# Values of all batches projected as their distinct context rows: three row sets in place of four batches, a layout by transfers, and a new order of the beginning

## The chip, the core and the metric

The kernel is one program on one core of a Trainium2 chip. A core has a matrix engine (PE, with its weight loads PEld shown apart), a vector engine (DVE), a scalar engine (ACT), a general engine (POOL) and a queue engine (SP), which here only starts transfers. Each of them works through its own list of instructions in order and meets the others at semaphores. The metric is the device time of one launch in microseconds (us), the median of several runs.

## The reference

Cross attention with a residual and a layer normalisation: 4 batches of 2048 query rows, 77 context rows per batch, width 512, 16 heads of 32.

```python
qs  = (q @ wq).reshape(Bq, Lq, H, HD).transpose(0, 2, 1, 3)      # q: (4, 2048, 512)
ks_ = (k @ wk).reshape(Bq, Lk, H, HD).transpose(0, 2, 1, 3)      # k = v = context: (4, 77, 512)
vs  = (v @ wv).reshape(Bq, Lk, H, HD).transpose(0, 2, 1, 3)
scores = jnp.einsum('bhqd,bhkd->bhqk', qs, ks_) / jnp.sqrt(jnp.float32(HD))
scores = jnp.where(mask[:, None, :, :], -jnp.inf, scores)
attn_w = jax.nn.softmax(scores, axis=-1)
attn = jnp.einsum('bhqk,bhkd->bhqd', attn_w, vs).transpose(0, 2, 1, 3).reshape(Bq, Lq, H * HD)
out = attn @ wo + q
mu = jnp.mean(out, axis=-1, keepdims=True)
var = jnp.mean((out - mu) ** 2, axis=-1, keepdims=True)
return (out - mu) / jnp.sqrt(var + EPS) * gamma + beta
```

## The kernel before

The 8192 query rows are 64 tiles of 128 rows. Two tiles make a block (256 rows, 32 of them), four make a group (512 rows, 16 of them). All large products are made in three passes of a format with fewer bits: each operand is cast (the high part, on ACT) and the rest is taken off it (the low part, on DVE or POOL), and high·high, low·high and high·low are added up in one PSUM bank. One product of 128 x 128 by 128 x 512 over a contraction of 512 is therefore 12 matmuls.

Nothing is scheduled by a compiler. The text `ORDER` is a list of some 2090 words, and the program emits the work in the order of these words, so that each engine gets its own words in their order. A word is a letter and a number. The letters that matter here:

- `A`, `C`, `F`: load the value weights wv in four slabs (SP), cast them while they are transferred (a transfer that POOL starts), take the low part (DVE). `R`, `p`, `G`: the same for the output weights wo, which take over the buffers `woh` and `wol` once the keys are projected with wk from them. `g`, `l`, `i`, `j`: load half a group of transposed x (`xT`), cast it on ACT (`xth`, L259), take its low part on POOL (`xtl`, L263).
- `H`, `Q`: projections of queries (L269); a `Q` is 12 matmuls of 512 columns, `I` and `q` copy the result out on DVE (L283, L285). `K`, `J`: copies of projected keys out of PSUM to `kct`, on ACT (L305) and on DVE (L307).
- `B`: values of one batch, 12 matmuls (L325). `D`: their copy out of PSUM (L332).
- `S`: scores of a tile, 64 small matmuls (L388). `T`: maxima of four heads with the mask's bias (DVE, L405). `e`: four exponentials and their sums (ACT, L420). `r`, `n`, `t`: reciprocals (DVE), scaling (POOL, L435), transposition in blocks of 32 (DVE, L456, into `B`).
- `P`: one of 12 transfers that regroup a block's transposed probabilities from `B` to `PT` (SP, L467). `V`: their product with the values of the block (L481). `a`, `b`: high and low part of it (ACT L510, DVE L514). `x`: load of the rows of x for the residual, `O`: the output projection (L534), `+`, `s`, `v`, `k`, `f`, `w`: residual, moments, the root (POOL), scale (ACT), the affine part (POOL), the store.

The second text, `SLOTS`, names the buffer that each tile takes, tag by tag: "mm" are the 8 PSUM banks, "o" the 8 row buffers, "xth" and "xtl" the two buffers of cast x.

A block's probabilities stand on 96 partitions: 77 keys for the even head of a pair and 77 for the odd one, the odd one's last 19 shifted in front or behind, so that a block of 32 is shared. The context is therefore loaded with its last 19 rows a second time (96 columns for each batch). The values are projected from these 96 columns, one batch at a time, and each copy out of PSUM multiplies the rows by a column of zeros and ones (`vm`, made at the start by `value_rows`): in the even heads the rows from 77 on are zero, in the odd ones the rows 58 to 76.

```python
def values_evac(b, a):
    pv = vd[b][:NK2].rearrange("p (q a d) -> p q a d", a=2, d=HD)
    vv = vsb[:, b].rearrange("p (q a d) -> p q a d", a=2, d=HD)
    nc.vector.tensor_scalar(vv[:, :, a], pv[:, :, a], vm[:, a, 0:1], None, ALU.mult)
```

The kernel ahead of the words (all of it in the listing below) loads the first rows of x, wq, the context and wk, projects the first 256 query rows and the keys; the words begin when the keys are projected. From tile 18 on the words repeat in a pattern of one block: two scores, one product with values, two projections of queries and two output projections.

Of the kernel before, what the change touches and what calls it, by code (L numbers as in the profile page):

```python
# [17 lines left out]
P = 128  # L18
# [13 lines left out]
GRP = 2 * BLK  # L32
MASKED = -3.38e38
# [5 lines left out]
LATE = 48  # L39

# [3 lines left out]
A0 A1 A2 A3 E l0 l2 C0 C1 C2 C3 g4 R2 g5 x1 J1 R1 M1.3 H2 K0 R3 p J3 K2 Y1 M0.1 R0 i2 i3 j2 S1 I2 S0 T1.1 e1.1 T1.3  # L44
j3 H0 T0.2 e0.2 T0.0 T0.1 e0.1 M8.4 F2 Q6 T0.3 e0.3 T1.2 I0 e0.0 T1.0 Q5 q6 i4 F0 r0 F3 e1.0 n0 S2 q5 e1.3 S3 T2.1
T2.3 j4 e1.2 Q4 t0 i5 F1 g6 Q7 r1 M4.4 T2.0 n1 T3.1 T3.3 e3.3 B2 j5 t1 e2.0 T3.0 P0.7s e3.1 P0.4s B1 D2.1 g7 G0
e3.0 x3 G1 x5 q4 P0.3s e2.3 T2.2 x4 B0 D1.0 P0.5s q7 i6 P0.6s M12.4 G2 e2.1 P0.9s D1.1 j6 P0.1s T3.2 S4 e2.2 D0.0
P0.2s T4.2 B3 P0.0s i7 r2 T4.1 P0.8s n2 e3.2 T4.0 P0.10s T4.3 P0.11s S5 e4.3 D3.0 g8 t2 Q11 x7 e4.0 L1 D2.0 T5.0
e4.2 r3 D0.1 n3 Q8 q11 e4.1 T5.1 D3.1 T5.2 e5.0 Q9 q8 T5.3 e5.3 r4 G3 t3 n4 e5.1 S6 P1.10s T6.3 V0 e6.3 P1.0s j7 q9
P1.8s T6.0 e5.2 P1.5s T6.1 S7 P1.6s T6.2 Q10 a0.0 t4 P1.2s e6.0 P1.9s P1.7s T7.3 a0.1 P1.3s e6.2 r5 T7.1 n5 Q13 x0  # L50
b0.1 P1.4s T7.2 e7.2 b0.0 t5 e6.1 O1 T7.0 P2.5s i8 q10 P1.1s q13 e7.0 P1.11s S8 P2.9s +1 r6 e7.1 P2.4s S9 T8.0 n6
P2.6s T8.2 O0 P2.8s e7.3 T8.3 P2.10s T8.1 g9 e8.1 t6 Y0 P2.11s Q15 P2.7s T9.2 e9.2 P2.0s T9.0 P2.1s r7 T9.1 n7 e8.3
P2.2s +0 V1 P2.3s s1 e8.2 T9.3 j8 t7 S10 a1.0 e8.0 Q12 b1.0 P3.2s T10.0 e9.3 x2 q15 P3.7s s0 P3.10s a1.1 Q14 e9.1
P3.8s r8 T10.3 v0 P3.3s T10.1 g11 e9.0 n8 T10.2 x6 b1.1 P3.11s O3 q12 e10.0 P3.4s r9 n9 t8 k0 e10.3 q14 V2 +3 f0 t9
a2.0 S11 a2.1 b2.0 k1 P4.5s O2 T11.1 P3.9s i9 T11.3 P4.11s e10.1 T11.2 j9 P3.5s b2.1 P4.9s e11.3 O5 P3.6s +2 P3.0s
s3 f1 e11.1 s2 M16.4 e10.2 S12 +5 T12.0 Q16 e11.2 v1 w1 r10 T12.1 P3.1s T12.3 n10 g10 k2 s5 P4.0s k3 O4 P4.2s q16
e12.1 P4.10s T11.0 f3 P4.1s e11.0 P4.4s w0 V3 +4 P4.7s T12.2 e12.2 P4.3s r11 t10 n11 w3 S13 P4.6s a3.0 a3.1 Q17 s4
P4.8s e12.3 T13.2 f2 b3.1 e12.0 b3.0 t11 O6 i10 v2 T13.0 e13.2 P5.0s r12 P5.3s T13.1 n12 P5.1s k5 S14 P5.8s k4
T14.0 O7 x9 e13.0 T14.2 f5 P5.2s T13.3 P5.5s e14.0 q17 w2 +6 V4 +7 e13.3 j10 w5 s7 P5.4s T14.3 P5.10s S15 a4.1 t12
P5.7s e13.1 f4 Q19 P5.9s P5.6s a4.0 T15.2 e14.3 x8 s6 x11 b4.0 P5.11s v3 Q18 T15.3 x13 r13 T14.1 N x10 e14.1 n13  # L60
b4.1 q19 e14.2 O9 T15.0 T15.1 k7 t13 e15.3 f7 O8 q18 P6.7s r14 e15.0 w4 +9 P6.2s s9 P6.4s i11 n14 w7 S16 +8 k6
P6.10s e15.2 T16.1 V5 P6.6s j11 T16.0 P6.1s T16.2 e16.1 x12 s8 S17 P6.0s P6.3s a5.0 T16.3 v4 Q20 e15.1 P6.9s t14
P6.11s f6 k9 P6.8s T17.0 P6.5s a5.1 T17.2 Q21 e16.2 g12 r15 b5.1 x15 n15 b5.0 e16.3 T17.3 T17.1 O11 e16.0 M20.4 q21
f9 e17.0 t15 O10 e17.3 q20 P7.7s r16 w6 +11 n16 i12 P7.2s s11 P7.4s k8 S18 w9 +10 e17.2 j12 P7.10s T18.1 V6 P7.6s
# [80 lines left out]
        "03762310475304714356170247102743062152346501256043120647150"  # L145
    ),
    "q": "1010101010101010",
    "xth": "1010101010101010",
    "xtl": "1010101010101010",
    "xtf": "010101010110101010101010101010",  # L150
    "PT": "1010101010101010101010101010101010",
# [16 lines left out]
def xattn_layernorm(  # L168
# [373 lines left out]
    def residual(t):  # L542
        nc.vector.tensor_tensor(od[t], pos.pop(t), od[t], ALU.add)  # L543
# [186 lines left out]
```

## Time and profile before

| | |
|---|---|
| median of 3 runs | 521.2 us (521.06 to 522.1) |
| the profiled execution's own time | 521.43 us |
| its span | 519.4 us |
| granted clock of the matrix engine | 0.998 |
| busy: PE, DVE, ACT, POOL | 507.8, 480.3, 460.2, 406.0 us |
| matmuls of the values | 48, from 39.5 us to 51.8 us |
| first exponential | 23.02 us |
| scores of tile 18 begin | 148.33 us |

The profile's span runs from the first to the last instruction; 2.0 us of the execution's time lie outside it. Busy time of PE covers the pipelined duration of matmuls (about 0.39 us for 512 columns), not the distance at which they follow each other, so what a matmul costs is read from the chain of work, where 36 of them take 8.30 us.

### The profile page before, as it was taken

To read this page: it belongs to the slowest core of one execution; us is meant where nothing else is said; L and a number is where in the kernel's file an instruction comes from. 1 tells how busy PE (TensorE), PEld (TensorE's weight loads), DVE (VectorE), ACT (ScalarE), POOL (GpSimd) and SP (SyncE) were. 2 spreads that over 40 slices of the span, in tenths; PEclk is the share of its full clock that TensorE was granted. 3 is DMA by queue.
4 is the path that set the end of the run, shared out by engine and by line. 5 is a ranking of instruction groups with operands and counts; after the bars stand their busy time and mean duration, and the time that the engine had idled before them with its cause. 6 is when DMAs were issued, how large, how long until landed. Compare 5 with 4: busy or idle time off the path is not lost.

```text
span 519.4 us, 20351 instructions
## 1 busy us (share of the span) xinstructions
PE 507.8 (98%) x6857; PEld 389.0 (75%) x6857; DVE 480.3 (92%) x2587; ACT 460.2 (89%) x2215; POOL 406.0 (78%) x368
## 2 busy tenths in 40 slices
PE   8999999999999999999999999999999898999995
PEld 6986787777777777777777787777777676667673
DVE  5798999979999999999999999999999999999997
ACT  6689999998999999999999999999999899988410
POOL 0655536898988998988888998988889689787652
PEclk9999999999999999999999999999999999999999
DMA  8957479677687786877777787877878575876863
GB/s 303 398 186 184 131 176 224 173 203 229 182 226 210 220 231 196 212 236 207 224 223 211 214 228 200 235 210 223 233 196 238 146 204 146 245 204 191 245 210 148
DMA packets 58583, 110.38 MB, mean 213 GB/s; under 512 B 9392, under 2 KB 11056, under 8 KB 58480
## 3 DMA queue, kind: packets, MB, share of 16 engines
q1 hardware_dynamic: 55024, 102.27, 68.6%
q0 software_dynamic: 2496, 5.77, 4.0%
q8 instruction: 54, 0.88, 0.8%
q10 hardware_dynamic: 960, 1.05, 0.7%
q14 instruction: 49, 0.40, 0.3%
HBM read 41.94 MB, written 16.78 MB: 113 GB/s over the span
## 4 chain that ended last, share of the span: by engine, by line
PE 63%; DVE 22%; POOL 5%; DMA 4%; SPq 2%; issue 2%; ACT 1%; DVEq 0%; POOLq 0%
PE pq L269 26%; PE po L534 19%; PE sc L388 8%; PE pa L481 7%; DVE pbuf L405 5%; DVE B L456 5%; DVE AL L514 2%; PE pv L325 2%; DVE o L589 2%; DVE st L576 2%; DVE o L586 2%; PE pk L292 1%; POOL pbuf L435 1%; DVE o L543 1%; DMA stage_a<-wk 1%
## 5 line engine op out<-in xcount | busy, mean ns | idle before, releaser
L420 ACT ACTIVATE pbuf<-pbuf,nm 128x77 f32<-128x77 f32 x1024 | 352.6, 351 | 11.5 <-DVE nm L405 11.5
L420 ACT ACTIVATION_READ_ACCUMULATOR pbuf<-pbuf,nm 128x1 f32 x1024 | 196.0, 191 | 0.0
L405 DVE CUSTOM_DVE_ANT_0 pbuf<-sc,mb 128x77 f32<-128x77 f32 x1024 | 171.3, 232 | 9.2 <-PE sc L388 5.1
L435 POOL TENSOR_TENSOR pbuf<-pbuf,ri 128x1232 f32<-128x1232 f32 x63 | 143.1, 2272 | 37.8 <-DVE ri L430 37.2
L269 PE MATMUL pq<-xth,wqh 128*128 128x512 f32 (+1 forms) x256 | 101.7, 397 | 1.3 <-DVE nm L405 1.1
L534 PE MATMUL po<-woh,AH 128*128 128x512 f32 x256 | 102.5, 400 | 0.0
L534 PE MATMUL po<-woh,AL 128*128 128x512 f32 x256 | 100.0, 391 | 1.8 <-DVE AL L514 1.6
L534 PE MATMUL po<-wol,AH 128*128 128x512 f32 x256 | 99.7, 390 | 0.0
L269 PE MATMUL pq<-xtl,wqh 128*128 128x512 f32 (+1 forms) x256 | 98.3, 384 | 0.2 <-POOL rn L554 0.2
L269 PE MATMUL pq<-xth,wql 128*128 128x512 f32 (+1 forms) x256 | 98.1, 383 | 0.0
L456 DVE STREAM_TRANSPOSE B<-pbuf 128x1280 f32<-128x1280 f32 x64 | 96.1, 1502 | 1.5 <-DMA PT<-B 0.9
L405 DVE DVE_READ_ACCUMULATOR2_ANT nm<- 128x1 f32 x1024 | 84.4, 82 | 0.0
L263 POOL TENSOR_TENSOR xtl<-xtf,xth 128x1024 fp32r<-128x1024 f32 x28 | 67.4, 2406 | 6.0 <-ACT xth L259 6.0
L388 PEld LDWEIGHTS sc<-kct,q 32*64 32x64 f32 x4096 | 52.1, 130 | 24.6 <-issue 13.1
L568 POOL TENSOR_TENSOR o<-o,bet 128x512 f32<-128x512 f32 x48 | 62.6, 1305 | 3.8
L567 POOL TENSOR_TENSOR o<-o,gam 128x512 f32<-128x512 f32 x48 | 63.4, 1321 | 0.9 <-ACT o L563 0.8
L388 PE MATMUL sc<-kct,q 32*64 32x77 f32 x4096 | 62.1, 238 | 0.6 <-DVE nm L405 0.5
L481 PE MATMUL pa<-PT,vsb 96*32 96x256 f32 x992 | 60.0, 382 | 0.0
L269 PEld LDWEIGHTS pq<-xth,wqh 128*128 128x128 f32 x256 | 48.0, 188 | 13.4 <-DVE nm L405 1.5
L534 PEld LDWEIGHTS po<-woh,AL 128*128 128x128 f32 x256 | 48.0, 188 | 13.2 <-DVE AL L514 3.1
L534 PEld LDWEIGHTS po<-woh,AH 128*128 128x128 f32 x256 | 48.1, 188 | 12.0 <-issue 1.8
L534 PEld LDWEIGHTS po<-wol,AH 128*128 128x128 f32 x256 | 48.1, 188 | 10.5 <-issue 1.0
(96 smaller groups left out, 661.4 us busy)
## 6 DMA issues: line engine op xcount, KB each, us to landing
PT<-B SPq DMA_DIRECT2D x343, 128.0 KB, 2.9
o<-x SPq DMA_DIRECT2D x64, 256.0 KB, 4.0
out<-o SPq DMA_DIRECT2D x64, 256.0 KB, 3.0
xtf<-xT SPq DMA_DIRECT2D x28, 512.0 KB, 4.2
PT<-B POOLq DMA_DIRECT2D x25, 128.0 KB, 3.3
xtf<-xT SPq DMA_DIRECT2D x4, 256.0 KB, 5.8
stage_a<-wq SPq DMA_DIRECT2D x4, 256.0 KB, 4.7
stage_a<-wk SPq DMA_DIRECT2D x4, 256.0 KB
```

Of the source, the lines that this page charges most:

```text
L263: nc.gpsimd.tensor_tensor(l[:, c : c + 2], fx.pop((g, c)), xh[g][:, c : c + 2].bitcast(F32), ALU.subtract)
L269: nc.tensor.matmul(pq, w[:, c, m * P : (m + 1) * P], r[g][:, c, rs], start=(n == 0), stop=(n == 11))
L325: nc.tensor.matmul(pv[:NK2, :], ctx_s[c][i][:, b, :], v[c], start=(n == 0), stop=(n == 11))
L388: mm = nc.tensor.matmul(sc[j][r0 : r0 + SR, g * NK : (g + 1) * NK], qs[q, g, rs.start + r0 : rs.start + r0 + SR], kct[q, g, t // TPB, keys ...
L405: nc.vector.tensor_tensor_reduce(pb[:, h // 2, (h % 2) * NK : (h % 2 + 1) * NK], scs[t][j][:, g * NK : (g + 1) * NK], mb[:, t % TPB, keys_ ...
L420: nc.scalar.activation(pb[:, h // 2, (h % 2) * NK : (h % 2 + 1) * NK], pb[:, h // 2, (h % 2) * NK : (h % 2 + 1) * NK], AF.Exp, bias=nmax[t ...
L435: nc.gpsimd.tensor_tensor(pv, pv, rv.to_broadcast((P, NP, 2, NK)), ALU.mult)
L456: nc.vector.transpose(bt.rearrange("p c q r -> p q c r"), pbuf[t % NPB].rearrange("p q (c r) -> p q c r", c=5),)
L481: nc.tensor.matmul(pas[b, g // 2][HD * j : HD * (j + 1), (g % 2) * BLK : (g % 2 + 1) * BLK], vsb[:, 2 * b // TPB, HD * h : HD * (h + 1)], ...
L534: nc.tensor.matmul(pos[t], a[:, c, rs], w[:, c, :], start=(first and c == 0 and n == 0), stop=(c == NC_D - 1 and n == 2),)
L567: nc.gpsimd.tensor_tensor(o, o, gam, ALU.mult)
L568: nc.gpsimd.tensor_tensor(o, o, bet, ALU.add)
```

## The change

1. **Context.** It is loaded without the repeated rows: 308 columns (4 x 77) in place of 384. The keys are projected from these 308 columns in place of 312.
2. **Values.** The 308 rows are projected as three sets of 128, 128 and 52 rows: 36 matmuls in place of 48. The columns of wv are reordered on the host, so that the even heads stand first. A set is copied out of PSUM whole (`values_evac`, three copies of 512 columns in place of eight of 256), into a row buffer, and 14 transfers (`place`, word `Z`, on SP) bring the rows to the partitions and batches where they belong in `vsb`. Rows that must be zero are set by three memsets on POOL ahead of everything; the memsets and the transposition on DVE that made `vm` are gone.
3. **Order.** The words up to the scores of tile 18 are written anew. From there on each engine's words are the same, one for one, as before. The words ahead of that point are the same ones on each engine, except `D` and `Z`, but stand in another order: batch sets 0, 2, 1; tile 6 ahead of tile 5 and 9 ahead of 8; blocks 0 and 1 multiplied with their values one right behind the other, block 3 ahead of block 2.
4. **Row buffers at the end.** The last eight tiles' rows of x (`LAST = 56`) are loaded into the buffers of cast x in place of the row buffers "o".

Some new helpers in the file (`hold`, `residual_late`, `shift_one`, `scale_one`, and the letters `*`, `#`, `@`, `%`, `o`) are used by no word.

On SP, ahead of the first two products with values. `PT` is a block's regrouped probabilities, `o` a tile's rows of x, `vsb` the values, `v` a projected set. Before:

```order
L365 DMA m_1_947<-mask 128x1536
L467 DMA PT_1063<-B_926 32x2x512 x9
L519 DMA o_1206<-x 128x512
L467 DMA PT_1063<-B_926 32x2x512
L467 DMA PT_1243<-B_1166 32x2x512
```

and in the changed kernel, from the load of x ahead of block 1's transfers to the load of xT behind them:

```order
L533 DMA o_940<-x 128x512
L343 DMA vsb<-v_880 19x256
L343 DMA vsb<-v_776 58x512
L478 DMA PT_1010<-B_913 32x2x512 x7
L343 DMA vsb<-v_776 19x256
L478 DMA PT_1010<-B_913 32x2x512 x2
L343 DMA vsb<-v_776 19x256
L478 DMA PT_1010<-B_913 32x2x512 x3
L262 DMA xtf_2_1177<-xT 128x1024
```

Four placements, three of them of batch 0, now stand among the twelve transfers of block 1.

On ACT, at the first words. `kct` are the keys (from the banks `pk`, in which the four parts lie; the scores begin with the first part), `xth` the cast x, the last row the first exponentials. Before:

```order
L305 ACTIVATE kct<-pk_232 128x4x77
L305 ACTIVATE kct<-pk_232 128x4x19
L305 ACTIVATE kct<-pk_234 128x4x77
L305 ACTIVATE kct<-pk_234 128x4x19
L259 CAST xth_347<-stage_a 128x1024 x2
L420 ACTIVATE pbuf_81,sum_430<-pbuf_81,nm_425 128x77 x4
```

and in the changed kernel:

```order
L311 ACTIVATE kct<-pk_226 128x4x77
L311 ACTIVATE kct<-pk_226 128x4x19
L265 CAST xth_332<-stage_a 128x1024
L311 ACTIVATE kct<-pk_224 128x4x77
L311 ACTIVATE kct<-pk_224 128x4x19
L265 CAST xth_332<-stage_a 128x1024
L431 ACTIVATE pbuf_80,sum_421<-pbuf_80,nm_416 128x77 x16
```

The third part of the keys is now copied first, and the first part (224) behind a cast of x that waits for its load (the second half of group 1).

On POOL, ahead of the low part of group 5's second half (`xtl`, the last row of both), which the projections `Q20` and `Q21` read. Before:

```order
L435 TENSOR_TENSOR pbuf_81<-pbuf_81,ri_2260 128x8x154
L567 TENSOR_TENSOR o_941<-o_941,gam 128x512
L568 TENSOR_TENSOR o_941<-o_941,bet 128x512
L435 TENSOR_TENSOR pbuf_82<-pbuf_82,ri_2329 128x8x154
L263 TENSOR_TENSOR xtl_2141<-xtf_2_1574,xth_2008 128x1024
```

and in the changed kernel:

```order
L446 TENSOR_TENSOR pbuf_81<-pbuf_81,ri_2172 128x8x154
L587 TENSOR_TENSOR o_1989<-o_1989,gam 128x512
L588 TENSOR_TENSOR o_1989<-o_1989,bet 128x512
L587 TENSOR_TENSOR o_1877<-o_1877,gam 128x512
L588 TENSOR_TENSOR o_1877<-o_1877,bet 128x512
L587 TENSOR_TENSOR o_1947<-o_1947,gam 128x512
L588 TENSOR_TENSOR o_1947<-o_1947,bet 128x512
L446 TENSOR_TENSOR pbuf_82<-pbuf_82,ri_2334 128x8x154
L269 TENSOR_TENSOR xtl_1996<-xtf_2_2011,xth_1821 128x1024
```

Two more tiles' affine parts stand between the two scalings.

The diff, cut to its core:

```diff
+PLACES = []
+for b in range(4):
+    cuts = sorted({0, NK - TAIL_K, NK} | {k for k in range(NK) if (b * NK + k) % P == 0})
+    for k0, k1 in zip(cuts, cuts[1:]):
+        PLACES += [(b, k0, k1, a) for a in ((None,) if k0 < NK - TAIL_K else (0, 1))]
...
 ORDER = """
-A0 A1 A2 A3 E l0 l2 C0 C1 C2 C3 g4 R2 g5 x1 J1 R1 M1.3 H2 K0 R3 p J3 K2 Y1 M0.1 R0 i2 i3 j2 S1 I2 S0 T1.1 e1.1 T1.3
+R1 R0 R3 E l0 l2 C2 C0 C1 C3 g5 M4.4 A0 M0.1 M12.4 A1 M1.3 A3 M8.4 K2 A2 H2 J3 p i3 g4 J1 K0 i2 S0 I2 j2 S1 T0.1
...
     for c in range(NC_D):
             for w, i in ((woh, 0), (woh, 1), (wol, 0)):
                 nc.tensor.matmul(
-                    pks[m][:, : NB * (NK + 1)],
+                    pks[m][:, : NB * NK],
...
-    def values(b):
-        pv = bank(f"pv_{b}")
+    def value_zeros():
+        for a, z0 in ((0, 64), (1, 32), (1, 64)):
+            nc.gpsimd.memset(vsb[z0 : z0 + 32, :, a], 0.0)
+
+    def values(g):
+        pv = vd[g] = bank(f"pv_{g}")
+        rows = slice(g * P, min(g * P + P, NB * NK))
         n = 0
         for c in range(NC_D):
             for i, v in ((0, wvh), (0, wvl), (1, wvh)):
-                nc.tensor.matmul(pv[:NK2, :], ctx_s[c][i][:, b, :], v[c], start=(n == 0), stop=(n == 11))
+                nc.tensor.matmul(pv[: rows.stop - rows.start], ctx_s[c][i][:, rows], v[c], start=(n == 0), stop=(n == 11))
                 n += 1
...
+    def values_evac(g, eng):
+        rows = min(P, NB * NK - g * P)
+        vr = vd[g, 1] = buf([P, D], F32, "o", name=f"v_{g}")
+        if eng is nc.scalar:
+            eng.copy(vr[:rows], vd.pop(g)[:rows])
+        else:
+            eng.tensor_copy(vr[:rows], vd.pop(g)[:rows])
+
+    def place(n, queue):
+        b, k0, k1, cols = PLACES[n]
+        g, r0 = divmod(b * NK + k0, P)
+        src = vd[g, 1][r0 : r0 + k1 - k0].rearrange("p (a d) -> p a d", a=2)
+        a = slice(0, 2) if cols is None else slice(cols, cols + 1)
+        z0 = k0 + TAIL_K if cols == 1 else k0
+        queue.dma_start(vsb[z0 : z0 + k1 - k0, b, a], src[:, a])
...
     def load_x(t):
-        od[t] = buf([P, D], F32, "o", name=f"o_{t}")
+        if t < LAST:
+            od[t] = buf([P, D], F32, "o", name=f"o_{t}")
+        else:
+            od[t] = once(ends, t // 4, [P, 4, D], F32, "xth" if t < LAST + 4 else "xtl")[:, t % 4]
...
-        nc.sync.dma_start(ctx_f[:, c : c + 2], ctxT[:, c : c + 2])
+        nc.sync.dma_start(ctx_f[:, c : c + 2, : NB * NK], ctxT[:, c : c + 2])
...
-    value_rows()
+    value_zeros()
```

More of the change, by code (lines that the diff above doesn't have):

```diff
@@ L39 @@
 LATE = 48
+LAST = 56
 ORDER = """
[L44 to L48 removed]
@@ L59 @@
[L59 to L63, printed above, removed]
```

265 lines of the change are left out of this document (136 added, 129 removed).

## The prediction

> **What bounds the kernel now.** I read the page's first part, then the busy time by stage, then the chain of work, and last the waits of each engine in the stage that the change rewrites.
>
> ```profile
> span 519.4 us, 20351 instructions
> PE 507.8 (98%) x6857; PEld 389.0 (75%) x6857; DVE 480.3 (92%) x2587; ACT 460.2 (89%) x2215; POOL 406.0 (78%) x368
> ...
> GB/s 303 398 186 184 131 176 224 173 203 229 182 226 210 220 231 196 212 236 207 224 223 211 214 228 200 235 210 223 233 196 238 146 204 146 245 204 191 245 210 148
> ...
> 20.00:145.00 125.00, 124.66 (x1779) 96.78 (x1778) 113.79 (x690) 116.12 (x581) 89.42 (x66) 1.00 0.72 197
> 145.00:400.00 255.00, 255.00 (x3619) 198.33 (x3621) 239.07 (x1341) 249.10 (x1190) 229.08 (x190) 1.00 0.77 219
> 480.00:500.00 20.00, 20.00 (x132) 14.05 (x131) 19.83 (x56) 8.06 (x37) 13.19 (x23) 1.00 0.76 222
> ```
>
> The columns of a stage's row are its length, then busy time (and instructions) of PE, PEld, DVE, ACT, POOL, the granted clock and the share and rate of the transfers. From 20 to 400 us PE has no gap worth a name; ACT is next, with 8.9 us idle up to 145 us and 5.9 us in the 255 us behind it. Towards the end DVE has no gap. The chain says the same:
>
> ```profile
> 11.98 7.01 PE pk L292 x46
> 39.66 8.30 PE pv L325 x36
> 48.85 2.95 PE pv L325 x12
> 102.48 5.11 DMA xtf<-xT
> 127.27 1.90 ACT pbuf L420 x11
> 132.59 2.26 POOL pbuf L435
> 134.84 2.34 POOL xtl L263
> 137.51 5.38 PE pq L269 x23
> 148.33 0.88 PE sc L388 x52
> 149.21 1.86 PE pa L481 x32
> 384.40 0.91 PE sc L388 x53
> 387.27 0.62 DVE st L548
> ```
>
> (start, length, what). It is PE from 12 to 94 us and from 137.5 to 385 us, and DVE with a little POOL behind that. Between 94 and 137.5 us the chain runs over transfers, DVE, ACT and POOL, though PE is busy there too: at 137.5 us the projection Q20 had to wait for the low part of x, so PE and the others reach that point almost together. That is the weak spot of every gain ahead of it.
>
> The end is held by DVE, but DVE comes there at PE's pace:
>
> ```profile
> DVE o L543 <- PE po L534: 7.7, 17, 0.8
> DVE pbuf L405 <- PE sc L388: 2.8, 16, 0.3
> ...
> PE pq L269 <- POOL rn L554: 0.2, 1, 0.2
> PE pk L292 <- DVE wol L243: 0.2, 1, 0.2
> ```
>
> The first two rows are DVE's waits from 150 to 400 us (total, times, longest): about once in a block it waits for PE. So what PE gains ahead of tile 18 moves the repeated part and the end with it.
>
> **The change part by part.** The sum is made against the profiled execution, 521.43 us (span 519.4 and 2.0 outside it); the median 521.2 us is 0.2 lower.
>
> *Values.* 36 matmuls in place of 48. In the chain 36 of them take 8.30 us and 12 take 2.95 us with the switch from the scores ahead, so one costs 8.30 / 36 = 0.231 us and twelve 2.77 us. PE has nothing else to do in their place and no gap: the whole of it is on the path. **-2.8 us.** That the third set has 52 rows in place of 128 saves nothing that I count, since all 12 matmuls still have 512 columns.
>
> *Keys.* 308 columns in place of 312: 7.01 us x 4 / 312 = **-0.1 us**, on the path. The context's two transfers of 384 KB shrink by a fifth, 154 KB in all; at the 398 GB/s that the row of transfer rates above shows for the second 13 us that is 0.4 us less ahead of wk. What it can free on PE is the 0.2 us wait for `wol` quoted above: **-0.2 us**.
>
> *First scores.* The third part of the keys is copied first, then ACT takes a cast that waits for the second load of group 1, then the first part, which every score needs. The rows of before:
>
> ```profile
> 17.71 0.55 ACT L305 ACTIVATE kct<-pk 128x308 f32<-128x308 f32 x2 [2.13 <-PE pk L292]
> 21.43 1.05 ACT L259 CAST xth<-stage_a 128x1024 fp32r<-128x1024 f32 x1 [1.36 <-DMA stage_a<-xT]
> 21.79 1.75 PE L388 MATMUL sc<-kct,q 32*64 32x77 f32 x128
> 23.02 0.36 ACT L420 ACTIVATE pbuf<-pbuf,nm 128x77 f32<-128x77 f32 x1 [0.54 <-DVE nm L405]
> ```
>
> If that load lands at 21.43 us as now, the cast (1.05) and the keys' copy (0.9) put the scores at 23.4, 1.6 us late, and PE has only them next. But ahead of it in the queue now stand three slabs of 256 KB in place of four and 154 KB less context: 0.41 MB, 1.0 us at 398 GB/s, and twice that if the casting transfers that POOL starts take half of the rate. So 0 to +1.6 us, and I take **+0.3**, nearer to none.
>
> *DVE.* Eight copies with the mask column go, three plain ones come:
>
> ```profile
> L332 DVE TENSOR_SCALAR vsb<-pv,small x8: 386/476/480, 42.5 to 56.9; 96x256 f32<-96x256 f32 x8
> L283 DVE COPY q<-pq 128x512 f32<-128x512 f32 x60 | 40.1, 669 | 1.8 <-PE pq L269 1.6
> ...
> POOL small L341 <- DMA stage_a<-wk: 11.5, 1, 11.5
> ```
>
> 8 x 0.46 - 3 x 0.67 = 1.7 us less of work, and the memsets and the transposition at 1 to 2 us fall into time in which DVE waits for loads. DVE has 11.2 us idle from 20 to 145 us: nothing on the path, but it helps the others be in time. The three memsets on POOL lie in its first wait of 11.5 us.
>
> *Placements.* 14 more issues on SP. SP starts a regroup transfer every 0.63 us when nothing holds it, so they take 8.8 us of a queue that the regroup transfers share:
>
> ```profile
> 152.44 3.79 SPq L467 DMA_DIRECT2D PT<-B  x6
> ...
> PT<-B SPq DMA_DIRECT2D x15, 128.0 KB, 4.6
> PT<-B SPq DMA_DIRECT2D x120, 128.0 KB, 2.6
> ```
>
> The last two rows give issue to landing, from 44 to 66 us and from 60 to 200 us. Four placements stand among block 1's twelve transfers, which V1 needs, and V1 now follows V0 at once. Behind the last of these transfers the order has two groups of exponentials ahead of V0 (eight in all; eleven chain rows of an exponential and its issue are five and a half of them in 1.90 us, so 2.8 us on a busy ACT), and V0 itself takes 1.9 us like the product at 149.21 us: 4.7 us, as much as the landing of 4.6. The other ten have at least a batch's time. No gain is possible; the loss goes from 0 to some 5 us (a rival below). I take **0**, because the second landing row already leaves 2 us.
>
> *The rest of the order.* PE's words up to tile 18 are the same but for one values set, with equally many switches to scores and products. Its work cannot shrink further; it can only be made to wait. Two things can do it:
>
> ```profile
> ACT pbuf L420 <- DVE nm L405: 6.8, 8, 2.4
> ...
> L567 POOL TENSOR_TENSOR o<-o,gam 128x512 f32<-128x512 f32 x4 | 5.2, 1296 | 0.8 <-ACT o L563 0.8
> ```
>
> ACT's work up to tile 18 does not change, so PE can come 2.8 us earlier only if ACT idles 6.1 us and not 8.9 us from 20 to 145 us. The new order brings tiles 2 and 3 one pair of projections earlier, which goes against the longest wait of 2.4 us; walking through the first four tiles with these durations I find ACT without a gap. And on POOL two more affine parts (2 x 1.3 us each) now stand ahead of the scaling and the low part that Q20 waits for: Q20 already waits 0.2 us, and from the scaling of tile 13 on POOL needs 2.3 + 3 x 2.65 + 2.3 + 2.4 = 15 us, while PE needs four of its 12-matmul blocks, two scores and a product, also 15 us. Bounds: -0.2 (the wait goes) to +2.8 (nothing arrives earlier); I take **+0.2**.
>
> *Row buffers at the end.* The loads of the last eight tiles no longer wait for stores. The end is DVE's, which never waits for them: 0, between -0.5 and 0.
>
> Sum: -2.8 - 0.1 - 0.2 + 0.3 + 0.2 = -2.6 us, so 518.8 us for the profiled execution and **518.6 us** for the median.
>
> **The rivals.**
>
> *The others do not follow (A).* PE saves its 2.8 us and waits for most of it at Q20, because ACT's 8.9 us of idle do not shrink or POOL's three affine parts come late. For it: the chain between 94 and 137 us, which today is already as long as PE's. Against it: the first waits of ACT are those that the order undoes. If 2 us are lost: 520.5 us.
>
> *The placements hold PE up (B), the slower one.* Should a placement move through few of the 16 DMA engines, then at 398 / 16 = 25 GB/s for one engine the 58 rows of 2 KB take up to 4.8 us there, and block 1's pieces on that engine queue behind. V1 then comes late by 4.8 us, PE has nothing to do between V0 and V1, and the time is 518.6 + 4.8 = 523.4 us. It turns into slower when V1 waits more than 3.6 us. The rows above speak on neither side: all transfers of the trace have 32 or 128 rows. Against it: seven transfers' issue time (4.4 us) lies between the placement of 58 rows and the next one, in which the engine can catch up. The Trainium skill (DMA: Bandwidth & Descriptors, on why a DMA increments its semaphore by 16) says that a transfer started by SP runs on the largest number of engines up to 16 that divides the rows on both sides, which for 58 is 2 and for 19 is 1. By that rule, which no run here shows yet, an estimate for the 58 rows is 2.4 us on two engines and the sum would be between 518.6 and 521.0 us.
>
> *The gain does not reach the end (C).* If DVE at 385 us were held by its own backlog, the time would stay 521.2 us. Its waits for PE up to 400 us speak against it.
>
> *More (D).* If the wait at Q20 and the load's lateness vanish and the end gains from its buffers, 521.2 - 3.1 - 0.2 - 0.5 = 517.4 us.
>
> **How the numbers follow.** Forecast 0.53, A 0.23, B 0.12, C 0.05, D 0.07. 0.2% is 1.04 us, about what a measurement of this kernel can tell from no change. Faster (under 520.2): the forecast, D and over half of A, 0.74. Same: C and the rest of A, 0.13. Slower: B and a little of A, 0.13. The range goes down to D's value, 517.4 us, and up to 521.3 us, which takes in A and C and leaves out B; the likeliest case's own range is 517.8 to 519.6 us.
>
> **What the profile after would show.** Chain: values in 36 matmuls, some 8.3 us. Waits: PE none above 0.5 us up to 145 us but at the first scores and at Q20. Stages: scores of tile 18 at 145.5 to 146 us in place of 148.33, the same distance from there to the end, ACT idle some 6 us from 20 to 145 us. I would be wrong if PE waits ahead of V0 or V1 for transfers (B), if Q20 waits 2 us (A), or if the first scores begin after 23 us.

## The result and the profile after

| | median | lowest to highest | runs |
|---|---|---|---|
| before | 521.37 us | 520.94 to 522.10 | 12 |
| changed | 521.65 us | 518.86 to 523.88 | 12 |

The ratio is 1.0003 with a 95% interval from 0.998 to 1.0026: no change of the median that can be told, where 518.6 us was forecast, and 0.35 us above the upper end of the range. What did change is the width. The times of the kernel before lie within 1.2 us of each other, those of the changed one are spread over 5 us.

The execution that was profiled is one of the short ones, 519.49 us. Its page and its chain of work (start, length, what), with the rows that answer to those shown of before:

```profile
span 517.7 us, 20315 instructions
...
PE 504.8 (98%) x6845; PEld 387.4 (75%) x6845; DVE 478.0 (92%) x2572; ACT 459.6 (89%) x2215; POOL 408.6 (79%) x371
...
DMA packets 59262, 110.86 MB, mean 214 GB/s; under 512 B 9430, under 2 KB 11758, under 8 KB 59158
```

```profile
12.15 6.73 PE pk L298 x48
21.79 1.86 PE sc L399 x92
39.79 2.72 PE pv L326 x12
44.33 5.69 PE pv L326 x24
109.45 2.66 DMA o<-x
112.11 0.67 DVE o L557
116.22 0.75 PE sc L399 x40
117.28 0.40 PE sc L399 x17
146.25 0.89 PE sc L399 x53
```

The values are there in 36 matmuls, the first scores begin at 21.79 us as before, and the chain no longer passes through the wait for Q20. The scores of tile 18 begin 2.1 us earlier (148.33 before). From there to the end it takes as long as before: 521.43 - 148.33 = 373.1 us, and 519.49 - 146.25 = 373.2 us. (In the profiles of e1, e2, e6, e7, e8, e14 and e15 below it is 372.7 to 373.5 us.) So what differs between these executions lies ahead of tile 18. One new place shows even here: DVE adds a tile's residual only when a load of rows of x has landed (112.11). The chain's row names the load that was issued at 109.45 us, but the semaphore that DVE waits for is that of the load before it, the rows of tile 4, issued at 106.97 and landed at 111.96 us. From there the chain comes from DVE to PE at 116.22, and the scores of a tile are torn in two there, with 0.3 us between the pieces.

### The profile page after: what moved, and what is told of

Its sections match the earlier page's. It is cut to its first block, busy times and chain, and to the rows that moved or that the text cites. A ratio compares the mean times of both kernels' runs of the same rounds, so it can differ in the third digit from the quotient of the medians.

```text
span 517.7 us, 20315 instructions
## 1 busy us (share of the span) xinstructions
PE 504.8 (98%) x6845; PEld 387.4 (75%) x6845; DVE 478.0 (92%) x2572; ACT 459.6 (89%) x2215; POOL 408.6 (79%) x371
## 4 chain that ended last, share of the span: by engine, by line
PE 63%; DVE 22%; POOL 4%; DMA 4%; issue 3%; SPq 2%; ACT 1%; DVEq 0%; POOLq 0%
PE pq L275 26%; PE po L548 19%; PE sc L399 8%; PE pa L492 6%; DVE pbuf L416 5%; DVE B L467 5%; POOL pbuf L446 2%; DVE AL L525 2%; DMA PT<-B 2%; DVE st L596 2%; PE pv L326 2%; SPq L478 1%; DVE o L617 1%; PE pk L298 1%; DVE o L557 1%
## 5 line engine op out<-in xcount | busy, mean ns | idle before, releaser
L431 ACT ACTIVATION_READ_ACCUMULATOR pbuf<-pbuf,nm 128x1 f32 x1024 | 198.1, 193 | 0.0
L548 PEld LDWEIGHTS po<-woh,AH 128*128 128x128 f32 x256 | 48.1, 188 | 12.7 <-issue 2.7
```

The lines of the kernel that those rows point to most:

```text
L431: nc.scalar.activation(pb[:, h // 2, (h % 2) * NK : (h % 2 + 1) * NK], pb[:, h // 2, (h % 2) * NK : (h % 2 + 1) * NK], AF.Exp, bias=nmax[t ...
L548: nc.tensor.matmul(pos[t], a[:, c, rs], w[:, c, :], start=(first and c == 0 and n == 0), stop=(c == NC_D - 1 and n == 2),)
```

## The experiments

Each group (e1 to e4, e5 to e8, e9 to e12, e13 to e15) was measured on one chip together with the kernel before, whose median was 521.2 to 521.6 us every time. The last column is the ratio to it with its 95% interval; runs of different groups are best compared by it.

| run | median | lowest to highest | ratio |
|---|---|---|---|
| e1_again | 521.22 | 519.13 to 523.56 | 0.9992 (0.9979 to 1.0006) |
| e2_oldends | 520.98 | 518.79 to 522.47 | 0.9983 (0.9968 to 0.9999) |
| e3_sixteen | 518.72 | 518.13 to 519.74 | 0.9948 (0.9936 to 0.9960) |
| e4_noplace | 517.48 | 517.31 to 518.48 | 0.9930 (0.9918 to 0.9942) |
| e5_split | 523.63 | 522.28 to 526.83 | 1.0056 (1.0034 to 1.0078) |
| e6_fixb1 | 519.50 | 517.90 to 523.38 | 0.9969 (0.9952 to 0.9986) |
| e7_fixb0 | 521.55 | 518.01 to 523.06 | 0.9999 (0.9981 to 1.0016) |
| e8_extra12 | 520.55 | 520.10 to 522.51 | 0.9990 (0.9981 to 1.0000) |
| e9_prime | 527.99 | 525.76 to 532.29 | 1.0120 (1.0093 to 1.0146) |
| e10_x4 | 524.25 | 523.40 to 527.19 | 1.0062 (1.0042 to 1.0082) |
| e11_x4_z | 531.83 | 528.17 to 533.90 | 1.0195 (1.0165 to 1.0224) |
| e12_x4_z_r2_k0 | 523.68 | 521.52 to 525.93 | 1.0045 (1.0022 to 1.0068) |
| e13_pieces | 519.09 | 517.85 to 522.50 | 0.9960 (0.9943 to 0.9976) |
| e14_r2_k0 | 521.30 | 518.74 to 523.76 | 0.9992 (0.9975 to 1.0008) |
| e15_pieces_r2_k0 | 518.66 | 517.78 to 519.92 | 0.9948 (0.9934 to 0.9961) |

### Does the width belong to the kernel, and to its end?

My theory now was the rival B of the prediction: placements that go through few DMA engines. Its own rivals were the row buffers at the end, the loads at the start, and the chip. First the changed kernel again, without an edit:

> The changed kernel once more, nothing edited. Its 12 times lay between 518.9 and 523.9 us, those of the kernel before between 520.9 and 522.1. If that width belongs to the kernel (placements on few DMA engines, or the loads at the start), the times are again 4 to 5 us wide, with a median of 519.5 to 523.5 us, and the profile, if it meets a long execution, has a stretch between 20 and 145 us that is 2 to 5 us later than the first profile (scores of tile 18 then after 148 us, 146.25 us in the first). If the width was that of one chip on one occasion, the times are within 1.2 us of each other, near 519.5.

Then with the old row buffers for the last eight tiles:

```diff
-LAST = 56
+LAST = 64
```

> The changed kernel with the rows of x of the last eight tiles in the row buffers again, as before; all else is as changed. Theory that the end is to blame for the width: the times come within 1.2 us of each other and the scores of tile 18 do not matter. Theory that placements or the start are to blame: the times stay 4 to 5 us wide, the median within 0.5 us of the changed kernel, at 0 to 0.5 us more.

Both are 4 us wide again, at 521.22 and 520.98 us: the width is the kernel's, and the buffers at the end have no part in it. The executions that were profiled took 520.47 and 521.64 us. Tile 18's scores in the chain of e1, then of e2:

```profile
147.11 0.89 PE sc L399 x53
```

```profile
148.51 0.88 PE sc L399 x53
```

DVE's wait for rows of x between 60 and 150 us (total, times, longest) in the first profile of the changed kernel, in e1, and in e2, there with a wait of PE for a placement:

```profile
DVE o L557 <- DMA o<-x: 1.4, 1, 1.4
```

```profile
DVE o L557 <- DMA o<-x: 1.7, 1, 1.7
```

```profile
PE pa L492 <- DMA vsb<-v: 0.7, 1, 0.7
...
DVE o L557 <- DMA o<-x: 2.1, 1, 2.1
```

Three profiles of 519.49, 520.47 and 521.64 us have tile 18 at 146.25, 147.11 and 148.51 us, and DVE's wait for rows of x grows with them: 1.4, 1.7, 2.1 us. That is 0.7 us more, where the times differ by 2.2 us, so this wait is only a part. The longest of the three also waited for a placement, at the products of blocks 0 and 1.

Another part is the matrix engine's clock, whose granted share is on record for every execution. Of the 24 executions of the unedited changed kernel (the first twelve and e1), ten took less than 521 us, with a mean clock of 0.996 to 0.998; seven took more than 522 us, and six of these have 0.994 or 0.995. The 87 executions of the kernel before in the four groups all have 0.996 to 0.999. In every profile the clock is at half for the last few microseconds, so a mean a little under 1 says nothing (e2's profile has 0.996 by that alone). But five profiles further below show what can lie behind a lower one: in e6, e9, e10, e11 and e12 the clock falls to half in the middle too, for 3.4 us or a multiple of it, behind waits of PE that add up to some 2 us or more. The stage from 60 to 100 us in the first profile of the changed kernel, then in e6, where the clock is at half from 58.9 to 62.3 us (the third column from the end is the clock):

```profile
60.00:100.00 40.00, 40.00 (x570) 30.51 (x554) 37.27 (x214) 38.58 (x195) 25.34 (x18) 1.00 0.74 196
```

```profile
60.00:100.00 40.00, 39.95 (x600) 30.16 (x599) 35.59 (x211) 35.47 (x178) 22.61 (x17) 0.97 0.70 182
```

Within such stretches matmuls of 512 columns follow each other by 0.43 us, outside by 0.23 us; by these two numbers a stretch of 3.4 us costs some 1.6 us of PE's time (an estimate). So a late transfer is paid for twice when PE's wait for it is followed by half the clock. Not every wait is: the profiles of e5 and e7 have waits as long, and no such stretch. None of the three profiles above has one either.

### Are the placements to blame, and by their engines or by their number?

All 14 with 16 or 32 rows, and then none:

```diff
-        queue.dma_start(vsb[z0 : z0 + k1 - k0, b, a], src[:, a])
+        m = 32 if k1 - k0 > 32 else 16
+        queue.dma_start(vsb[z0 : z0 + m, b, a], vd[g, 1].rearrange("p (a d) -> p a d", a=2)[:m, a])
```

> Every one of the 14 placements moves 16 or 32 rows (the first rows of its set) in place of 58, 51, 33, 25, 19 or 7, to the same first partition, so the number of transfers and their places in the queue stay; the values on the other rows are zero, set by one memset over the whole of the layout, so the products with values are of other numbers. Theory of placements on few engines (58 and 19 rows bring 2 and 1 semaphore packets in place of 16): the times become 1 to 1.5 us wide and the median 518.5 to 519.5 us. Theory of the start or of the order: width and median stay as in the changed kernel, 521.7 us and 4 to 5 us wide.

```diff
-        queue.dma_start(vsb[z0 : z0 + k1 - k0, b, a], src[:, a])
+        del src
...
-        for a, z0 in ((0, 64), (1, 32), (1, 64)):
-            nc.gpsimd.memset(vsb[z0 : z0 + 32, :, a], 0.0)
+        nc.gpsimd.memset(vsb, 0.0)
```

> The 14 placements are left out, and the layout of the values is zero (one memset), so the output is the residual path alone. Theory of placements, whatever way they hurt: 518.0 to 519.5 us, within 1.5 us of each other. If the number of transfers and not their engines matters, this one is narrow and the one with 16 and 32 rows is not. Theory of the start or of the order: 521.7 us, still 4 to 5 us wide.

518.72 us and 517.48 us, 1.6 and 1.2 us wide. The layout by transfers costs 521.22 - 517.48 = 3.7 us on this chip, of which 521.22 - 518.72 = 2.5 us go when as many transfers move rows by 16 and 32. They also move fewer rows; the runs e9 (fewer rows, fewer engines) and e13 (all rows, more engines) below tell the two apart. The packets under 512 B in the four pages count why. Before, then changed, then with 16 and 32 rows, then with none:

```profile
DMA packets 58583, 110.38 MB, mean 213 GB/s; under 512 B 9392, under 2 KB 11056, under 8 KB 58480
```

```profile
DMA packets 59353, 110.69 MB, mean 214 GB/s; under 512 B 9617, under 2 KB 11921, under 8 KB 59249
```

```profile
DMA packets 58839, 110.22 MB, mean 214 GB/s; under 512 B 9392, under 2 KB 11568, under 8 KB 58736
```

Without placements there are 9392, as before the change; with the 14 placements of 16 and 32 rows 225 more (16 for each make 224; the one left over is not explained); in the changed kernel only 38 more. The Trainium skill (DMA: Bandwidth & Descriptors, on why a DMA increments its semaphore by 16) says that a transfer's engines are the largest number up to 16 that divides its rows, and that each of them posts one write. For 58, 19, 19, 51, 7, 19, 19, 58, 19, 19, 25, 33, 19 and 19 rows that is 2+1+1+3+7+1+1+2+1+1+5+11+1+1 = 38. The trace agrees to the packet.

And without placements PE waits for no transfer. All its waits between 40 and 400 us in e4, then tile 18 in e4's chain:

```profile
PE pv L325 <- PE sc L398: 0.2, 1, 0.2
```

```profile
144.57 0.88 PE sc L398 x53
```

### Fewer engines still

```diff
-        queue.dma_start(vsb[z0 : z0 + k1 - k0, b, a], src[:, a])
+        m = {58: 53, 51: 47, 33: 31, 25: 23}.get(k1 - k0, k1 - k0)
+        queue.dma_start(vsb[z0 : z0 + m, b, a], src[:m, a])
```

> The placements of 58, 51, 33 and 25 rows move 53, 47, 31 and 23 rows (prime numbers), the others are as changed, so there are as many transfers and about 9% fewer bytes; a few rows of the values stay zero. Theory of few engines (rows that no number up to 16 divides go through one): the load of rows of x behind the placement of 47 rows lands later by the time of 47 packets of 2 KB on one engine in place of 17 on each of three, 30 x 0.08 to 0.13 = 2.4 to 4 us, and the median is 523 to 525 us; the profile has 25 or so fewer packets under 512 B than the changed kernel (14 placements on one engine each, but the one of 7 rows on 7: 20 in place of 38). Theory of bytes or of the number of transfers: 521.4 us as before.

527.99 us, some 6.5 us more than the changed kernel although fewer bytes move: more than expected (523 to 525), in the direction that only the theory of few engines allows. The small packets are 20 more than before, as counted ahead. The profiled execution is the longest of the six, 532.29 us, and its clock is at half for 10.2 us from 122.0 us on, behind a wait of PE of 5.6 us, so a good part of its price (some 4.8 us by the two distances above) is the clock's. The shortest execution, 525.76 us, has a mean clock of 0.998, as high as any of the changed kernel's under 521 us, and is still 4.5 us above the changed kernel's median. The row of the profile's page, then the longest waits of PE and DVE for transfers, and SP's two longest for placements:

```profile
DMA packets 59226, 110.82 MB, mean 209 GB/s; under 512 B 9412, under 2 KB 11740, under 8 KB 59122
```

```profile
PE sc L399 <- DMA PT<-B: 5.6, 1, 5.6
...
DVE o L557 <- DMA o<-x: 7.2, 1, 7.2
...
SPq L478 <- DMA vsb<-v: 6.2, 2, 5.4
...
SPq L364 <- DMA vsb<-v: 3.8, 1, 3.8
```

The times from issue to landing, worked out from the trace's records of semaphore updates (start us, what, us from there to its landing):

```
changed    53.88  58 rows on 2 engines     6.45
           55.59  regroup, 128 KB, behind  5.32
           69.54  58 rows on 2 engines     7.40
          105.41  51 rows on 3 engines     4.73
          106.97  rows of x, tile 4        4.99
e9_prime   54.84  53 rows on 1 engine      8.10
           70.26  31 rows on 1 engine      8.11
           70.99  23 rows on 1 engine      8.93
           71.61  53 rows on 1 engine     12.73
          110.19  47 rows on 1 engine     10.75
          111.59  rows of x, tile 4       10.23
```

Two things are seen. A transfer of 128 rows that stands behind a placement lands just behind it: the rows of tile 4 after 10.23 us behind 47 rows on one engine, after 4.99 us behind 51 rows on three (5.2 us more, where 2.4 to 4 were expected), while the three loads of rows of x between 100 and 110 us take a median of 2.7 us without placements (row of the transfers' view of e4):

```profile
o<-x SPq DMA_DIRECT2D x3, 256.0 KB, 2.7
```

The regroup transfers behind the 47 rows land as late, at 121.2 to 122.5 us, and PE's wait of 5.6 us, which ends at 122.4 us, is put down to them. And three placements on one engine each, issued within 1.4 us, land one behind the other, at 78.4, 79.9 and 84.3 us, so it looks like the same engine. The Trainium skill says that too, in the same section of that page: a transfer that SP starts takes the lowest-numbered of the 16. The records here don't name engines. The last two of these landings also give a pace: 53 rows of 2 KB in 84.34 - 79.92 = 4.42 us, 25 GB/s. The 47 rows took longer, 7.59 us from the landing of the 19 rows ahead of them (113.35 us) to their own (120.94 us), 13 GB/s; what makes the difference is not shown.

The last two rows of waits, SP's own, are a cost that I had not thought of. SP's transfers take turns at eight semaphores, and each waits for the one before it on its semaphore to have landed. The load of gamma is the eighth transfer behind the 53 rows at 71.61 us and could start only at 84.36 us, when they had landed; every regroup transfer behind it waited along. The regroup transfer that is the eighth behind the 47 rows waited 5.4 us in the same way and started at 120.95 us. In the changed kernel SP loses 0.8 us at the same load.

### Which of the placements?

```diff
+        if n in (3, 6):          # e6: batch 1; e7: (0, 1, 2, 13), ahead of block 1's product
+            m, src = (32 if m > 32 else 16), vd[g, 1].rearrange("p (a d) -> p a d", a=2)
```

> Only the placement of 51 rows (batch 1, 3 engines) and the last one of 19 rows of that batch move 32 and 16 rows; the other twelve are as changed; the rest of the layout is zero, so these rows are missing in the products. Both stand ahead of loads of rows of x on SP at 104 to 106 us. Theory that this place costs the more: DVE no longer waits 1.4 to 2.1 us for rows of x near 110 us, and the median is 519.0 to 520.0 us with half the width. If the place ahead of the product of block 1 is the one: 520.5 to 521.5 us.

> Only the four placements ahead of the product of block 1 (58, 19 and 19 rows of batch 0 and 19 of batch 3) move 32 or 16 rows; the ten others are as changed; the missing rows are zero. If the two places add up, this run and the one that mends batch 1 alone save together what the run with all 14 mended saves (521.4 - 518.7 = 2.7 us): 520.0 to 521.0 us here, with the wait near 110 us still there in the profile and the two products of blocks 0 and 1 within 4.1 us of their start.

Batch 1's two placements alone give 519.50 us, as expected in the median (though not in the width), and DVE waits for no rows of x near 110 us in e6's profile. That is 1.7 us under e1's median, which is from another chip; by the ratios to the kernel before it is 0.23%, 1.2 us. The four ahead of block 1's product alone give nothing: 521.55 us. In the medians the two fall short of the 2.5 us of all 14, but with intervals of nearly 1 us on either side, and with eight placements that neither run mends, this does not show that they fail to add up. The wait of DVE near 110 us is one place where a gain can be lost; in e7 it is longer than in the three profiles above:

```profile
DVE o L559 <- DMA o<-x: 2.8, 1, 2.8
```

In e7's profile DVE is ready for tile 4's residual 0.7 us earlier than in the first profile of the changed kernel, but SP starts the load of these rows 1.1 us later, and they land 0.8 us later (112.75 and 111.96 us). What is gained ahead of this point is lost in waiting there, as long as the rows do not come earlier too.

The profiled execution of e6 was one of its longest, 521.99 us, and shows another new place. DVE's wait for a slab of the output weights in the timeline, and PE's behind it among the waits:

```profile
51.21 0.69 DVE L369 TENSOR_TENSOR wol<-stage_b,woh 128x512 fp32r<-128x512 f32 x1 [2.05 <-DMA stage_b<-wo]
```

```profile
PE pq L275 <- DVE nm L418: 1.8, 1, 1.8
```

The new order loads the third slab at 45 us, among block 0's transfers, where the old one has all four by 22 us. PE's wait ends at 58.2 us, and the stretch at half the clock follows it at 58.9 us.

### Is the saved work worth its price?

```diff
+        if g == 2:       # beside the placements left out: the third set's 12 matmuls twice
+            for c in range(NC_D):
+                for i, v in ((0, wvh), (0, wvl), (1, wvh)):
+                    nc.tensor.matmul(pv[: rows.stop - rows.start], ctx_s[c][i][:, rows], v[c], start=True, stop=True)
```

> The 14 placements are left out (the layout of the values is zero) and the third set's 12 matmuls are made twice, so PE has 48 matmuls for the values as before the change. If the matmuls are on the path with their whole time: 517.48 + 2.77 = 520.2 us. If ACT, DVE or POOL held the beginning as well: 518 to 519.5 us.

520.55 us against 517.48 us: 12 matmuls more cost 3.1 us (2.77 expected), on the path with their whole time. The two runs are from two chips; their ratios to the kernel before give 3.1 us too. Its profiled execution, at 522.51 us the longest of the ten, shows the late first scores that the prediction bounded (chain):

```profile
21.82 1.05 ACT xth L265
22.86 0.34 ACT kct L311
...
23.25 1.86 PE sc L402 x89
```

Here the load for the cast ahead of the keys' first part landed late, and the first scores began at 23.25 us: 1.5 us behind the first profile's 21.79.

### Attempts to mend it that failed

Every placement cut in two, the bulk by multiples of 16:

```diff
+        m = (k1 - k0) // 16 * 16
+        for r, r1 in ((0, m), (m, k1 - k0)):
+            if r < r1:
+                queue.dma_start(vsb[z0 + r : z0 + r1, b, a], src[r:r1, a])
```

> Every placement is cut in two: the rows up to the last multiple of 16 (48 of 58 and 51, 32 of 33, 16 of 25 and 19) and the rest, so that the bulk of the rows goes through 16 engines; all rows arrive as in the changed kernel, by 27 transfers in place of 14. Theory of few engines: the width falls to 1.5 us and the median to 518.5 to 519.5 us, near the run with 16 and 32 rows (518.72) although all the bytes are moved. Theory that the bytes or the number of transfers hold the work up: 521 us or more, since SP issues 13 more of them (some 8 us of SP).

523.63 us: slower, against my expectation. Thirteen more transfers at 0.6 us hold SP up, and regroup transfers land late, at block 1's product (68.8 us, the second row) and once more at 104.3 us. PE's longest waits:

```profile
PE sc L402 <- DMA PT<-B: 1.8, 1, 1.8
PE pa L495 <- DMA PT<-B: 1.4, 1, 1.4
```

So more transfers have a price of their own. How much of it is SP's time, and how much the rests of 1 and 3 rows, which still go through one and three engines, no run separates. Then words moved: the load of tile 4 ahead of batch 1's last placements, with that the three of batch 0 earlier (`Z1` and `Z2` are taken from their old places as `Z0` is), and with both the third slab loaded earlier, at some 36 us, and the keys' first part copied ahead of the cast:

```diff
-Z6.s T13.2 P4.4s e13.2 r11 Z3.s +6 n11 O7 P4.2s T13.1 a2.1 x4
+x4 Z6.s T13.2 P4.4s e13.2 r11 Z3.s +6 n11 O7 P4.2s T13.1 a2.1
```

> The changed kernel with one word moved: the load of the rows of tile 4 stands ahead of the placement of 19 rows at 104 us and so ahead of that and of the placement of 51 rows. Nothing else is edited. Theory that this load, landing 5 us after its issue behind the 51 rows, is the larger part: DVE has no wait for rows of x near 110 us, the median is 519.3 to 519.9 us, like the run with these two placements mended (519.5). If that run gained by something else: 521.4 us.

```diff
-P0.0s G0 B2 e3.1 R2
+P0.0s Z0.s Z1.s Z2.s G0 B2 e3.1 R2
...
-Z13.s t2 e6.0 Z0.s G1
+Z13.s t2 e6.0 G1
```

> As the run with the load of tile 4 moved, and the three placements of batch 0 stand right behind the copy of their set, among block 0's transfers (at some 46 us) and no longer among block 1's. Theory: the products of blocks 0 and 1 follow within 3.6 to 3.8 us, as without placements, and the median is 518.3 to 519.2 us. If the transfers of block 0 now come late ahead of the first product: 519.5 us or more.

```diff
-J3 p i3 g4 J1 K0
+J3 p K0 i3 g4 J1
...
-x1 T3.1
+x1 R2 T3.1
```

> As the run before it, and the two other places that the new order made tight are undone: the third slab of the output weights is loaded at some 37 us and not at 45 us (in one execution DVE waited 2.05 us for it at 49 us and 3.9 us were lost), and ACT copies the first part of the keys ahead of the cast that waits for its load (in one execution the first scores began at 23.25 us). Theory: these set the longest times, so the width falls to 1 us and the median to 517.7 to 518.7 us. If the moved load delays others: no gain over the run before it.

All three are slower than before, by 0.6, 2.0 and 0.5%. In e10 DVE's wait for tile 4 is gone, but the next tile's residual waits 3.1 us (the view puts it down to PE; the rows of that tile landed at 115.85 us, just ahead of its start at 115.93), PE waits 2.2 us for regroup transfers, and SP stands 3.1 us for stores:

```profile
PE sc L397 <- DMA PT<-B: 2.2, 1, 2.2
...
SPq L531 <- DMA out<-o: 3.1, 2, 2.2
...
DVE o L555 <- PE sc L397: 3.1, 1, 3.1
```

Tile 4's rows go to the buffer that tile 3 leaves, and tile 3's store had just been issued, at 102.78 us. The load could start only when it had landed, at 106.64 us, and SP's whole queue stood behind it: the load of tile 5 came at 111.34 in place of 109.45 us, and the 51 rows at 108.45 in place of 105.41 us, so that the regroup transfers behind them landed late for PE. Whose buffer the load takes had been left out of the expectation. In e11 the placements of 58 and twice 19 rows stand right ahead of the load of the third slab, and DVE pays for it:

```profile
DVE wol L365 <- DMA stage_b<-wo: 5.3, 1, 5.3
```

The slab landed 7.5 us after its issue, behind placements on two engines and one. 8 us of e11 go with e12's two edits, the earlier slab and the earlier copy of the keys; no run separates the two here. The clock, too, is at half in all three profiles, for 3.4 us in e10 and e12 and for 10.2 us in e11, so a part of these prices is its.

### More engines for nearly the same number of transfers

Every row is moved, in 17 pieces whose numbers of rows have large divisors; the tails of the odd heads keep their 19 rows, and two small pieces have 7 and 3:

```diff
+PIECES = {
+    0: ((0, 45, None), (45, 77, 0)), 1: ((45, 58, 1),), 2: ((58, 77, 1),),
+    3: ((0, 48, None), (48, 51, None)), 4: ((51, 58, 1),), 5: ((51, 77, 0),), 6: ((58, 77, 1),),
+    7: ((0, 45, None), (45, 77, 0)), 8: ((45, 58, 1),), 9: ((58, 77, 1),),
+    10: ((0, 25, None),), 11: ((25, 77, 0),), 12: ((25, 58, 1),), 13: ((58, 77, 1),),
+}
```

> All rows are placed as in the changed kernel, in pieces whose number of rows has a divisor near 16: for batch 0 and 2 45 rows of both halves (15 engines), 32 rows of the even half (16) and 13 of the odd one (13), the odd tails of 19 rows as before; 48, 3, 26 and 7 rows for batch 1; 25 (both), 52 and 33 for batch 3: 17 transfers in place of 14, at the same places in the order. Theory of few engines: 518.8 to 520.0 us, narrower than the changed kernel, no wait of DVE for rows of x near 110 us above 0.5 us, and some 178 packets under 512 B more than before the change where the changed kernel has 38 (19+15+16+13+19+11+13+5+15+16+13+19 and so on count as 1+15+16+13+1+11+13+5+15+16+13+1+13+7+1+16+3 = 160). Theory that any transfer more on SP costs as much: 521.4 us or more.

> The changed kernel, its placements as they are; the third slab of the output weights is loaded at some 37 us in place of 45, and ACT copies the first part of the keys ahead of the cast that waits. If these two places cost time in many executions: 520.0 to 520.8 us. If they do so only now and then: 521.0 to 521.6 us, with the highest times (523.9) gone.

> Both of the two edits before. If the effects add up: 0 to 1 us less than the run with the pieces alone, 518.2 to 519.6 us, within 1.5 us of each other.

(The 178 in the first of these is a slip; the sum written out is 160, and the page of the profile has 9552 - 9392 = 160.) The pieces alone give 519.09 us, 2.2 us under the 521.30 us of e14, which has the changed kernel's placements; ten of their twelve times lie between 517.85 and 519.66 us. The two places alone give nothing in the median, 521.30 us. Both together give 518.66 us and a width of 2.1 us (1.5 expected), 0.52% under the kernel before (0.39 to 0.66%): every row in its place, and faster than both kernels. In the last one 48 rows on 16 engines land after 2.93 us and the rows of tile 4 behind them after 2.65 us, by the same records as above. The highest times of the pieces alone (522.50 and 521.71) are not met by the five runs with both edits; that these come from the slab or the first scores, no profile of such an execution shows. Nor does the earlier copy of the keys rule out late first scores: in e15's profile, its longest execution (519.92 us), they begin at 23.49 us. There 18 of the 47 distances between the matmuls of the first projections are 0.21 us and not 0.12, all ahead of 10.4 us (4 in the first profile of the changed kernel), and the record of the full clock begins at 10.56 us and not at 3.85 us. So a clock that rises late delays the first scores as well as a load that lands late.

## Why the prediction was wrong

- **Values, -2.8 us: right.** Without placements the twelve matmuls are worth 3.1 us (e8 against e4), and what PE saves does reach the end: from tile 18 to the end it is 373.1 us before and 372.7 us in e4 (517.31 - 144.57). Rival C falls with it.
- **Keys and the wait for wol, -0.3 us: right.** The chain's row of the keys went from 7.01 to 6.73 us, and the wait is not among PE's.
- **First scores, +0.3 us: the bounds held, the usual value was 0.** 21.79 us in the first profile, as before; 23.25 us in one execution of e8.
- **Q20, +0.2 us, and rival A: wrong, for the better.** PE doesn't wait there in the first profile, nor in e4, where the others follow to the end. This with the 0.2 us that Q20 waited before, 0.3 us of the first scores and 0.3 us more for the values is 1.0 of the 1.1 us between the 518.6 us forecast and e4's 517.48 us. (Against the kernel before on its own chip, 521.56 us, e4 saves 4.1 us and not 3.7; these 0.4 us more are not accounted for.)
- **Row buffers at the end, 0: right** (e2 against e1: 0.2 us, within their intervals).
- **Placements, 0: the step that failed.** They cost 3.7 us in the median. "I take 0, because the second landing row already leaves 2 us" took the price of a transfer with 32 or 128 rows for one with 58, on 2 engines: it landed after 6.45 us, not 4.6 or 2.6, and the regroup behind it after 5.3. The sentence on the other ten, "have at least a batch's time", looked only at who reads the placed rows, and not at what stands behind the transfer on its engines: the rows of tile 4 behind batch 1's 51 rows, which landed after 4.99 us where they take 2.6 us without placements. One execution could have hidden this: the profiled one, 519.49 us, lies inside the forecast's range, and so do four others of the twelve.
- **Rival B was the mechanism, with a wrong price and mostly at another place.** Its 25 GB/s for one engine is the pace between two landings in e9, but not what a placement gets from its issue on: 53 rows of 2 KB took 8.10 us there on one engine, and the 58 rows 6.45 us on two, where 4.8 us were the most for one engine and 2.4 us the estimate for two. V1 lost 0.7 us for a placement in one profile and nothing in another; the larger part was lost behind batch 1's placements (e6: 1.2 to 1.7 us of the 2.5 that engines cost). The Trainium skill's rule, weighed there, had the engines right to the packet; "the sum would be between 518.6 and 521.0 us" by it counted only the 58 rows' own time.
- **"Its work cannot shrink further; it can only be made to wait. Two things can do it":** there was a third, the slab of the output weights, loaded 45 us into the kernel. It cost in one profiled execution of e6 (2.05 us of DVE) and, behind placements, in e11 (5.3 us). And a wait of PE is not all that it can cost: behind some waits the clock was at half, and the same matmuls took 0.43 us in place of 0.23.

What stays open in part is why one execution loses 1 us and the next 5. The profiles show where (the landings behind placements, the slab, the first scores), and the lower mean clock of six of the seven executions above 522 us speaks for a stretch at half the clock in them. The profiles do not show what makes the same transfer faster or slower from one execution to the next, and no profile met an execution of the unedited changed kernel above 522 us.

## What to carry to other kernels

A transfer between partitions is priced by how many DMA engines its number of rows lets it use, and that is read from the packets under 512 B: placements took 3.7 us of a saving of 4 us here, and 2.5 of these went when as many transfers ran on 16 engines, in place of two, one and three for 58, 19 and 51 rows. The bill comes to whatever stands behind it, on those engines and, eight transfers later, on SP, so ask for the next loads in the queue and not for the reader of the moved rows. Before a load is moved ahead, look whose buffer it takes: in an ordered queue, its wait becomes everybody's. And where times spread, compare the clock of the long executions with that of the short ones.

## What was not expected of the hardware

- A transfer of 128 rows landed as late as a small one on one engine ahead of it: after 10.23 us behind 47 rows on one engine, after 2.65 us behind 48 rows on 16.
- Placements on one engine each, issued together, landed one behind the other (8.1, 8.9 and 12.7 us after their issue).
- SP's next transfer on the same semaphore, eight behind, started only when the slow one had landed (84.36 us; the slow one was issued 12.7 us before), which makes a small transfer a stop for the queue.
- Thirteen more transfers, with most of the rows then on 16 engines, cost 523.63 - 521.22 = 2.4 us against the changed kernel's 14 (0.64%, 3.3 us, by the ratios).
- The matrix engine's clock was at half for stretches of 3.4 us (e6, e10, e12) up to 10.2 us (e9) behind waits of PE, with matmuls of 512 columns 0.43 us apart in place of 0.23.
